# Order of the first loads, larger portions of the edge count, and the place of the check and the split in a GNN and LSTM kernel

## The chip, the cores and the metric

The kernel runs as one program on one core of a Trainium2 chip. The metric is the device time of one execution in microseconds (us); the time of a kernel is the median of several runs. Five engines each take their own instructions strictly in the order in which the program lists them: PE (TensorE: matrix products, with weight loads listed apart as PEld), DVE (VectorE), ACT (ScalarE), POOL (GpSimd) and SP (SyncE, which issues transfers). They wait for each other through semaphores.

## What is computed

```python
def _gcn2_layer(h, h0, src, dst, norm, w1, w2, b, layer):
    beta = float(np.log(LAMBDA / layer + 1.0))
    x = h * norm
    agg = jax.ops.segment_sum(x[src], dst, num_segments=h.shape[0])
    agg = agg * norm
    f, f0 = agg * (1.0 - ALPHA), h0 * ALPHA
    return relu((1-beta)*f + beta*(f @ w1) + (1-beta)*f0 + beta*(f0 @ w2) + b)
...
h = layernorm(x) @ fc_w.T + fc_b                     # x: 1250 rows of 512
norm = clip(degree_of(dst), 1) ** -0.5               # 20000 edges, dst sorted
x = x + layer2(layer1(h))
x = x + lstm(layernorm(x))                           # 1250 steps, hidden size 512
```

A linear layer with a layer norm ahead of it, two graph layers over 20000 edges, and an LSTM over the 1250 rows, with residual sums. Only the part ahead of the first graph layer is touched by the change.

## The kernel before

The 1250 rows stand in T = 10 tiles of 128 partitions by 512. The sum over edges is made as a matrix product with an adjacency matrix of counts, `adj`, which the kernel builds itself on PE: for each of 160 groups of 125 edges, DVE makes two one-hot matrices, `ob` (line 287, source within a tile) and `od` (line 289, target and source tile), and PE multiplies them into one of 32 blocks of 40 target nodes in PSUM (line 303). A block is opened by a product with zeros (line 300). When its last group is in, it is closed (`close_block`, lines 194 to 199): ACT copies it into `adj`, and then DVE reduces it into `S`, the counts for each source tile. There are four PSUM buffers for blocks (`acc`), two for transposes (`psT`), two for products (`psM`, line 207), and eight buffers for one-hot matrices, which is two batches of four groups. `count(n)` (line 338) multiplies batch n, then has DVE make the one-hots of batch n + 2, then closes blocks.

In the first stage PE, DVE and ACT follow an order written out by hand (`manual_schedule`, line 240). A loop over slots s = 0 to 13 (line 358) takes tile s through these steps, a slot apart: PE transposes the normed tile (`xT`); PE multiplies it by the transposed weights `fcT` (`product`, lines 163 to 167, called in line 373) and DVE adds the bias into `h` (line 380); PE transposes `h` (line 378); PE makes two products with `w2` (line 389); DVE adds a bias to each of the two and so frees the two `psM` buffers, at the head of the next slot (lines 366 to 368). Between the steps stand three calls of `count`, one batch each, so that the 40 batches fill slots 0 to 12 and a part of slot 13.

Ahead of the loop DVE converts the edge lists, computes `low` and `key` from them (lines 246 to 275), makes the one-hots of two batches, and takes the layer norm statistics of tiles 0 and 1 (`stats(0, 2)`); `stats(2, 4)` stands in slot 0 and `stats(4, 10)` in slot 1. Each `stats` has one square root on ACT in its middle (line 88).

Transfers: the edge lists on SP and ACT; the rows of tile i on SP for even i and on ACT for odd i, two transfers a tile (`load_rows`, line 112), and four small ones on SP for the last four partitions (`load_last_rows`). POOL issues `fc_w` (1 MB), a bias, the two `w2` (1 MB each) and two biases, and makes `ids_f` (line 237) after them. A transfer on SP or ACT uses one of eight semaphores in turn and so waits until the eighth transfer before it has landed.

After the loop, with no hand-written order, come: the largest entry of `S` (line 432), the degrees as ten products of `S` with a column of ones (`count_edges`, line 397), the number of edges that were not counted (`missing`, lines 436 to 442), `norm` (line 403), and the split of the first layer's input, `h * norm`, into three bf16 planes for each tile (`split_input`, line 420: ACT writes the high plane, DVE the rest, ACT the middle plane, DVE the low one). Four of the ten tiles are split there. Then every engine reads `missing` into a register (line 446) and branches (line 858): with a missing edge to `general()`, otherwise, as here, to `fast()`, which lies behind it. There SP and POOL load the LSTM's input weights `Wx` (line 474), the other six tiles are split (line 674), and PE runs the first layer's sum over edges, `agg` (line 685): for each of four column blocks, 90 products over tiles in the order 6, 7, 8, 9, 0, 1, 2, 3, 4, 5, three planes each.

Of the kernel before, what the change touches and what calls it, by code (L numbers as in the profile page):

```python
# [17 lines left out]
ALPHA = 0.1  # L18
# [20 lines left out]
def gnn_lstm_kernel(  # L39
# [44 lines left out]
    def rsqrt(pool, v, name):  # L84

        w = v.shape[1]
        s = pool.tile([R, w], F32, name=name + "_s")
        nc.scalar.activation(s, v, AF.Sqrt)
        r = pool.tile([R, w], F32, name=name + "_r")
        nc.vector.reciprocal(r, s)  # L90
        q = pool.tile([R, w], F32, name=name + "_q")
        nc.vector.tensor_mul(q, r, r)
        nc.vector.tensor_mul(q, q, v)
        nc.vector.tensor_scalar(q, q, -0.5, 1.5, OP.mult, OP.add)
        nc.vector.tensor_mul(r, r, q)
        return r
# [4 lines left out]
    nc.vector.memset(ones, 1.0)  # L101

# [9 lines left out]
    def load_rows(i, dst):  # L112


        for p0, p1 in ((0, 16), (16, P - 1)):
            (nc.scalar if i % 2 else nc.sync).dma_start(
                dst[4 * p0:4 * p1, i, :],
                bass.AP(tensor=x.tensor, offset=x.offset + (LEN * p0 + 4 * i) * D,
                        ap=[[LEN * D, p1 - p0], [D, 4], [1, D]]))

    def load_last_rows(dst, fill):

        def rows(r, i0, i1, first, n):
            nc.sync.dma_start(dst[R - 4 + r:R - 4 + r + n, i0:i1, :],
                              bass.AP(tensor=x.tensor, offset=x.offset + first * D,
                                      ap=[[D, n], [4 * D, i1 - i0], [1, D]]))
# [19 lines left out]
    def layernorm_scale(pool, mv, name):  # L146
        ve = pool.tile([R, mv.shape[1]], F32, name=name + "_v")
        nc.vector.tensor_scalar(ve, mv[:, :, 1], EPS, None, OP.add)
        return rsqrt(pool, ve, name)
# [36 lines left out]
    with ExitStack() as gnn_stack:  # L186
# [6 lines left out]

        def close_block(p, i, dst):
# [6 lines left out]
        with tc.tile_pool(name="prep", bufs=1) as prep, \  # L201
# [13 lines left out]
            for i in range(T):  # L215
                load_rows(i, xt)
                if i == 0:
                    load_last_rows(xt, fill=True)
            fcw = prep.tile([128, KD, D], F32, name="fcw")
            nc.gpsimd.dma_start(fcw, fc_w.rearrange("(a p) i -> p a i", p=128))  # L220
            biases = []
            for name, v in (("fcb", fc_b), ("b1", b_1), ("b2", b_2)):
                b = prep.tile([R, D], F32, name=name)
                biases.append(b)
            fcb, *bl = biases
            nc.gpsimd.dma_start(fcb, row_bcast(fc_b, R))
            w2 = []
            for i, v in enumerate((w2_1, w2_2)):
                w = prep.tile([128, KD, D], F32, name=f"w2_{i}")
                nc.gpsimd.dma_start(w, v.rearrange("(k p) n -> p k n", p=128))  # L230
                w2.append(w)
            for b, v in zip(bl, (b_1, b_2)):
                nc.gpsimd.dma_start(b, row_bcast(v, R))
# [4 lines left out]
                           allow_small_or_imprecise_dtypes=True)  # L238

            with tc.manual_schedule(engines={mybir.EngineType.PE, mybir.EngineType.DVE,  # L240
                                             mybir.EngineType.Activation}):

# [11 lines left out]
                e_src, e_dst = ends  # L254
                none = edges.tile([ER, BW * T], F16, name="none")
# [54 lines left out]

                mv = prep.tile([R, T, 2], F32, name="mv")
                rstd = prep.tile([R, T], F32, name="rstd")
                nmr = prep.tile([R, T], F32, name="nmr")

                def stats(t0, t1):
                    for t in range(t0, t1):
                        layernorm_stats(work, mv, t, xt[:, t, :])
                    r = layernorm_scale(prep, mv[:, t0:t1, :], f"ln{t0}")
                    nc.vector.tensor_copy(rstd[:, t0:t1], r)
                    nc.vector.scalar_tensor_tensor(nmr[:, t0:t1], mv[:, t0:t1, 0], -1.0, r,  # L320
                                                   op0=OP.mult, op1=OP.mult)

# [9 lines left out]
                n_batch = EC // BATCH  # L332

# [4 lines left out]
                def count(n):  # L338
                    closed = []
                    for c in range(n * BATCH, min((n + 1) * BATCH, EC)):  # L340
                        closed += count_group(c)
                    onehots(n + 2)
                    for p, i in closed:
                        close_block(p, i, adj[:, :, :, 4 * i:4 * i + 4])

                onehots(0)
                onehots(1)
                stats(0, 2)
# [7 lines left out]
                normed(0)  # L356
                n = 0
                for s in range(T + 4):
                    if s < T:
                        xTs[s] = transposed(work, psT, xns.pop(s), "xT")  # L360
# [8 lines left out]
                    if n < n_batch:  # L369
                        count(n)  # L370
                        n += 1
                    if 0 <= s - 1 < T:
                        ps_h[s - 1] = product(psM, xTs.pop(s - 1), fcT)
                    if n < n_batch:
                        count(n)
                        n += 1
# [4 lines left out]
                    if n < n_batch:  # L381
                        count(n)
                        n += 1
# [6 lines left out]
                assert n == n_batch and not blocks  # L390


        deg = gnn.tile([R, T], F32, name="degs")
        norm = gnn.tile([R, T], F32, name="norms")
        norm9 = gnn.tile([R, T], F32, name="norm9")

        def count_edges(psD):
            pd = psD.tile([R, T], F32, name="deg")
            for t in range(T):
                nc.tensor.matmul(pd[:, t:t + 1], S[:, t, :], ones, start=True, stop=True)  # L400
            nc.vector.tensor_copy(deg, pd)

        def degree_norm(pool):
            nc.vector.tensor_scalar(deg, deg, 1.0, None, OP.max)
            r = rsqrt(pool, deg, "norm")
            nc.vector.tensor_copy(norm, r)
            nc.vector.tensor_scalar(norm9, norm, 1.0 - ALPHA, None, OP.mult)

        def split(v, rest, hi, mid, lo, scale=None):

            if scale is None:
                nc.scalar.copy(hi, v)
                nc.vector.tensor_sub(rest, v, hi)
            else:
                nc.scalar.activation(hi, v, AF.Copy, scale=scale)  # L415
                nc.vector.scalar_tensor_tensor(rest, v, scale, hi, op0=OP.mult, op1=OP.subtract)
            nc.scalar.copy(mid, rest)
            nc.vector.tensor_sub(lo, rest, mid)

        def split_input(pool, t, v, scale=None):  # L420
            rest = v if scale is None else pool.tile([R, D], F32, name="rest")
            split(v, rest, *(planes[:, t, i, :] for i in range(3)), scale=scale)

        chunks = [(6, 4), (0, 4), (4, 2)]
        order = [t for t0, n in chunks for t in range(t0, t0 + n)]
        assert sorted(order) == list(range(T))

        AHEAD = 4
        with tc.tile_pool(name="deg_ps", bufs=1, space=PSUM) as psD, \
                tc.tile_pool(name="deg_sb", bufs=2) as sbD:  # L430
            most = sbD.tile([R, 1], F32, name="most")
            nc.vector.tensor_reduce(most, S.rearrange("b i r -> b (i r)"),
                                    mybir.AxisListType.X, OP.max)
            nc.vector.tensor_scalar(most, most, 256.0, None, OP.is_gt)
            count_edges(psD)
            row = sbD.tile([R, 1], F32, name="row")
            nc.vector.tensor_reduce(row, deg, mybir.AxisListType.X, OP.add)
            nc.vector.tensor_sub(row, row, most)
            pn = psD.tile([1, 1], F32, name="total")
            nc.tensor.matmul(pn, row, ones, start=True, stop=True)  # L440
            missing = sbD.tile([1, 1], I32, name="missing")
            nc.vector.tensor_scalar(missing, pn, -1.0, float(E), OP.mult, OP.add)
            degree_norm(gnn)
            for t in order[:AHEAD]:
                split_input(sbD, t, h[:, t, :], norm[:, t:t + 1])
            n_missing = nc.values_load(missing, min_val=0, max_val=E + R)
# [35 lines left out]
        def load_x_again():  # L482
            load_last_rows(h, fill=False)
            for t in order:
                load_rows(t, h)
# [12 lines left out]
        def rstd_of(pool, t0, n):  # L498
            r = layernorm_scale(pool, mv2[:, t0:t0 + n, :], f"lx{t0}")
            nc.vector.tensor_copy(rstd2[:, t0:t0 + n], r)  # L500
# [94 lines left out]
        def general():  # L595


            with tc.tile_pool(name="any", bufs=1) as anyp, \
# [23 lines left out]
                count_edges(any_ps)  # L622
# [40 lines left out]
        def layers():  # L663
            with tc.tile_pool(name="gcn_all", bufs=1) as gcn1, \
# [8 lines left out]

                for t in order[AHEAD:]:
                    split_input(gcn, t, h[:, t, :], norm[:, t:t + 1])
# [216 lines left out]
```

## Time and profile before

| | us |
|---|---|
| median of 3 runs (1155.21 to 1156.94) | 1156.25 |
| the profiled execution | 1157.69 |
| its span, first to last instruction | 1155.9 |
| first stage, up to the last product of the edge count | 194.04 |
| check and branch, up to the first `agg` product | 203.89 |
| end of the first layer's `agg` | 278.60 |
| the second layer's `agg` | 312.99 to 377.84 |
| LSTM, from about | 557 |
| PE busy | 1025.9 (89%) |
| DVE busy | 519.3 (45%) |
| ACT busy | 344.4 (30%) |

A line of the timeline has start, duration, engine, line, operation, what it writes and reads, the count, and in brackets how long the engine stood idle before it and what ended that. A line of the chain of waits has a start, a duration and the work that the end of the program hung on then. fp32 products are recorded as two passes: one `product` of four is recorded as eight. "Granted clock" is the share of the throttle; a lower rate of the products themselves is seen only in their spacing.

### The profile page before, as it was taken

The page shows a single profiled execution, that of the slowest core. Times are in us where ns is not written, and L with a number is a line of the kernel's source. Part 1 is how long each engine was busy: PE and PEld are TensorE (multiplying, and loading weights), DVE is VectorE, ACT ScalarE, POOL GpSimd, SP SyncE. Part 2 cuts the span into 40 slices and gives each one's busy share as a digit, 9 for nine tenths or more (in the row PEclk, how much of TensorE's full clock was granted, in tenths as well). Part 3 has the DMA queues.
Part 4 walks back from the last instruction along what each step waited for, and adds up shares of the span by engine and source line. Part 5 has one row for each costly group of instructions (what it writes and reads, how often), then busy time and mean ns, then how long its engine had stood idle before and what let it go on. Part 6 is the DMA issues. An engine that isn't in the chain of part 4 may idle for free.

```text
span 1155.9 us, 27516 instructions
## 1 busy us (share of the span) xinstructions
PE 1025.9 (89%) x11340; PEld 535.2 (46%) x11356; DVE 519.3 (45%) x1775; ACT 344.4 (30%) x1284; POOL 69.8 (6%) x123
## 2 busy tenths in 40 slices
PE   2999997799999999999788888888888888888886
PEld 1555544355455444444344444444444444444443
DVE  4956665401500665555444444444434444443444
ACT  2312212412500023333333333333333333333332
POOL 1000000300000281000000000000000000010011
PEclk9999999799999999999999999999999999999999
DMA  8000000800300175222632323232322333333331
GB/s 233 1 1 1 1 1 2 256 1 1 89 1 1 69 168 181 109 110 109 199 97 84 97 84 98 84 98 84 94 87 87 95 88 94 102 97 102 102 102 21
DMA packets 41466, 96.22 MB, mean 83 GB/s; under 512 B 6125, under 2 KB 21846, under 8 KB 39928
## 3 DMA queue, kind: packets, MB, share of 16 engines
q1 hardware_dynamic: 35012, 77.59, 22.3%
q0 software_dynamic: 4496, 14.09, 4.2%
q10 hardware_dynamic: 1819, 2.65, 0.8%
q8 instruction: 92, 1.51, 0.6%
q14 instruction: 47, 0.38, 0.1%
HBM read 71.93 MB, written 19.76 MB: 79 GB/s over the span
## 4 chain that ended last, share of the span: by engine, by line
PE 67%; DVE 16%; ACT 9%; issue 4%; DMA 3%; POOL 0%; DVEq 0%; ACTq 0%; SPq 0%
PE gates L540 28%; PE psM L166 15%; PE agg L685 11%; PE psM L510 10%; DVE pr L553 3%; ACT th L556 3%; DVE hT L558 3%; DVE hh L557 3%; DVE cg L554 3%; ACT cg L547 3%; PE acc L303 2%; ACT sg L549 2%; DMA base<-in_x_dram 2%; DMA bx<-in_L_ffn_b_i_dram 1%; PE psT L155 1%
## 5 line engine op out<-in xcount | busy, mean ns | idle before, releaser
L540 PE MATMUL gates<-Wh,hT 128*32 128x256 f32 x8320 | 482.5, 383 | 75.2 <-DVE hT L558 75.2
L540 PEld LDWEIGHTS gates<-Wh,hT 128*32 128x32 f32 x8320 | 244.7, 110 | 287.1 <-DVE hT L558 151.9
L553 DVE TENSOR_TENSOR pr<-sg,cg 128x128 f32<-128x128 f32 x260 | 70.6, 272 | 223.9 <-ACT sg L549 223.8
L685 PE MATMUL agg<-adj,planes 128*128 128x512 bf16 (+1 forms) x704 | 134.6, 352 | 10.0 <-ACT planes L415 7.2
L510 PE MATMUL psM<-Wx,xT 128*128 128x512 f32 x320 | 138.7, 594 | 1.5 <-ACT xT L160 1.5
L547 ACT ACTIVATE cg<-gates 128x64 f32<-128x64 f32 x260 | 58.2, 224 | 249.2 <-PE gates L540 245.6
L556 ACT ACTIVATE th<-cg 128x64 f32<-128x64 f32 x260 | 66.7, 256 | 138.6 <-DVE cg L554 138.6
L685 PEld LDWEIGHTS <-planes 128*128 128x128 bf16 x720 | 71.8, 100 | 73.0 <-ACT planes L415 7.6
L557 DVE TENSOR_TENSOR hh<-so,th 128x64 f32<-128x64 f32 x260 | 58.6, 225 | 86.4 <-ACT th L556 86.0
L510 PEld LDWEIGHTS psM<-Wx,xT 128*128 128x128 f32 x320 | 60.4, 190 | 76.8 <-issue 72.9
L558 DVE STREAM_TRANSPOSE hT<-hh 128x64 f32<-128x64 f32 x260 | 63.8, 246 | 27.9 <-DVE hh L557 0.9
L166 PE MATMUL psM<-w,hT 128*128 128x512 f32 x160 | 70.9, 596 | 0.0
L549 ACT ACTIVATE sg<-gates 128x128 f32<-128x128 f32 x260 | 70.5, 271 | 0.2
L554 DVE TENSOR_TENSOR cg<-pr 128x64 f32<-128x64 f32 x260 | 58.5, 225 | 8.9
L806 POOL TENSOR_TENSOR base<-base,hh 128x128 f32<-128x128 f32 x40 | 18.4, 461 | 693.0 <-issue 533.4
L551 ACT ACTIVATE so<-gates 128x64 f32<-128x64 f32 x260 | 59.8, 230 | 0.0
L532 PE MATMUL gates<-xs,sel 96*32 96x256 bf16 x1040 | 52.5, 272 | 4.2 <-DMA xs<-xp_d 4.2
L303 PE MATMUL acc<-od,ob 125*128 125x400 f16 (+22 forms) x360 | 47.9, 260 | 9.0 <-DVE od L289 8.2
L289 DVE TENSOR_SCALAR od<-ids,key 125x820 f16<-125x820 f16 (+42 forms) x160 | 55.6, 347 | 0.0
L287 DVE TENSOR_SCALAR ob<-ids,low 125x128 f16<-125x128 f16 x160 | 39.5, 247 | 16.3 <-PE acc L303 16.0
L166 PEld LDWEIGHTS psM<-w,hT 128*128 128x128 f32 x160 | 29.7, 190 | 34.0 <-issue 33.0
L303 PEld LDWEIGHTS <-ob 125*128 125x128 f16 x360 | 29.7, 98 | 31.6 <-issue 12.7
(154 smaller groups left out, 663.6 us busy)
## 6 DMA issues: line engine op xcount, KB each, us to landing
xs<-xp_d SPq DMA_DIRECT2D x130, 384.0 KB, 3.2
xp_d<-planes SPq DMA_DIRECT2D x10, 1536.0 KB, 5.4
w<-in_L_gnn_w_dram POOLq DMA_DIRECT2D x4, 1024.0 KB, 12.8
xp_d<-adj POOLq DMA_DIRECT2D x1, 1440.0 KB, 7.8
base<-x SPq DMA_DIRECT2D x20, 64.0 KB, 2.3
base<-x POOLq DMA_DIRECT2D x20, 64.0 KB, 2.6
fcw<-in_L_gnn_fc_w_dram POOLq DMA_DIRECT2D x1, 1024.0 KB, 8.6
out_dram<-base SPq DMA_DIRECT2D x12, 64.0 KB, 2.2
```

Of the source, the lines that this page charges most:

```text
L166: nc.tensor.matmul(p, lT[:, k, :], rhs[:, k, :], start=(k == 0), stop=(k == KD - 1))
L303: nc.tensor.matmul(blocks[i][:, (d0 - i * BW) * T:(d1 - i * BW) * T], ob, od[:, (d0 - lo) * T:(d1 - lo) * T], start=False, stop=last)
L510: nc.tensor.matmul(p, yT[:, k, :], Wx[:, k, j, :, :], start=(k == 0), stop=(k == KD - 1))
L540: nc.tensor.matmul(ps[s][32 * j:32 * (j + 1), :, :], hT[b // 2][:, b % 2, :], Wh[:, b, j, :, 64 * s:64 * (s + 1)], start=False, stop=(b == 3))
L547: nc.scalar.activation(cg[:, 1, :], p[:, 3, :], AF.Tanh)
L549: nc.scalar.activation(sg, p[:, 0:2, :], AF.Sigmoid)
L553: nc.vector.tensor_mul(pr, sg, cg)
L554: nc.vector.tensor_add(cg[:, 0, :], pr[:, 0, :], pr[:, 1, :])
L556: nc.scalar.activation(th, cg[:, 0, :], AF.Tanh)
L557: nc.vector.tensor_mul(hh[:, m], so, th)
L558: nc.vector.transpose(hT.rearrange("p b c -> p (b c)"), hh[:, m])
L685: nc.tensor.matmul(p[:, :n * R], planes[:, k, pl, f * 128:(f + 1) * 128], adj[:, k, t0:t0 + n, :].rearrange("b i r -> b (i r)"), start=(k ...
```

## The change

Loads: `fc_w` goes first on POOL, then `ids_f`, then the three biases. All rows of x go on SP, tiles 0 and 1 first, then 2 and 3, then tiles 4 to 9 together in eight transfers; behind them the two `w2`, also on SP. The four small transfers go on ACT. A square root of a constant on ACT comes ahead of them. `stats(0, 2)` and `normed(0)` move ahead of the one-hots and of `ids`. `rsqrt` writes its last product where it is wanted, so that a copy goes.

Counting: instead of three batches in each slot there are 3 in slot 0, 4 in slots 1 to 8 (1, 2 and 1), 3 in slot 9 and 2 in slot 10.

Check and split: they move into slots 10 to 13, behind those slots' products, in the hand-written order, and all ten tiles are split there. The tiles that they use move to other pools.

```diff
+    warm = keep.tile([128, 1], F32, name="warm")
+    nc.scalar.activation(warm, ones, AF.Sqrt)
...
+        def count_edges(pd):
+            for t in range(T):
+                nc.tensor.matmul(pd[:, t:t + 1], S[:, t, :], ones, start=True, stop=True)
+            nc.vector.tensor_copy(deg, pd[:, :T])
+
+        def row_totals():
+            nc.vector.tensor_reduce(most, S.rearrange("b i r -> b (i r)"),
+                                    mybir.AxisListType.X, OP.max)
+            nc.vector.tensor_scalar(most, most, 256.0, None, OP.is_gt)
+            nc.vector.tensor_reduce(row, deg, mybir.AxisListType.X, OP.add)
+            nc.vector.tensor_sub(row, row, most)
+
+        def total(pn):
+            nc.tensor.matmul(pn, row, ones, start=True, stop=True)
+            nc.vector.tensor_scalar(missing, pn, -1.0, float(E), OP.mult, OP.add)
...
             xt = base1
-            for i in range(T):
-                load_rows(i, xt)
-                if i == 0:
-                    load_last_rows(xt, fill=True)
             fcw = prep.tile([128, KD, D], F32, name="fcw")
             nc.gpsimd.dma_start(fcw, fc_w.rearrange("(a p) i -> p a i", p=128))
...
+            load_rows(0, 2, xt)
+            load_last_rows(xt, nc.scalar, fill=True)
+            load_rows(2, 4, xt)
+            load_rows(4, T, xt)
...
+                stats(0, 2)
                 none = edges.tile([ER, BW * T], F16, name="none")
...
+                normed(0)
                 onehots(0)
                 onehots(1)
-                stats(0, 2)
...
+                per_slot = [(1, 1, 1)] + [(1, 2, 1)] * 8 + [(1, 2, 0), (1, 1, 0)]
                 for s in range(T + 4):
+                    c0, c1, c2 = per_slot[s] if s < len(per_slot) else (0, 0, 0)
...
                     if 0 <= s - 4 < T:
                         for l, p in enumerate(ps_b.pop(s - 4)):
                             nc.vector.tensor_add(base[l][:, s - 4, :], p, bl[l])
-                    if n < n_batch:
-                        count(n)
-                        n += 1
+                    count(c0)
                     if 0 <= s - 1 < T:
                         ps_h[s - 1] = product(psM, xTs.pop(s - 1), fcT)
...
+                    count(c1)
                     if 0 <= s - 2 < T:
                         hTs[s - 2] = transposed(prep2, psT, h[:, s - 2, :], "hT")
                     if 0 <= s - 1 < T:
                         nc.vector.tensor_add(h[:, s - 1, :], ps_h.pop(s - 1), fcb)
...
+                    count(c2)
...
                     if 0 <= s - 3 < T:
                         hT = hTs.pop(s - 3)
                         ps_b[s - 3] = [product(psM, hT, w2[l]) for l in range(2)]
...
+                    if s == T:
+                        count_edges(psT.tile([128, KD, R], F32, name="psT")[:, 0, :])
+                        row_totals()
+                        degree_norm(prep)
+                    if s == T + 1:
+                        total(psT.tile([128, KD, R], F32, name="psT")[:1, 0, :1])
+                    for t in order[slice(*{T: (0, 2), T + 1: (2, 5), T + 2: (5, 8),
+                                           T + 3: (8, T)}.get(s, (0, 0)))]:
+                        split_input(prep2, t, h[:, t, :], norm[:, t:t + 1])
+        n_missing = nc.values_load(missing, min_val=0, max_val=E + R)
...
-                for t in order[AHEAD:]:
-                    split_input(gcn, t, h[:, t, :], norm[:, t:t + 1])
```

Also moved: before the second layer, x is loaded again into `h` in 20 transfers, all on SP now, where SP and ACT had ten each.

## The prediction

> **What bounds the kernel now.** I read the chain of waits first. From 41 us to the end it is almost all PE, so time is won only where PE stands still. That is the case ahead of 41 us and around 200 us, the two places that the change touches. The timeline of the start shows why:
>
> ```profile
> 17.02 0.17 DVE L90 RECIPROCAL ln_r<-ln_s 128x2 f32<-128x2 f32 x1 [1.88 <-ACT ln_s L88]
> 24.95 0.69 DVE L143 BATCH_NORM_STATS2 bnst<-base 128x6 f32<-128x512 f32 x1 [6.71 <-DMA base<-in_x_dram]
> 39.08 1.21 PE L303 MATMUL acc<-od,ob 125*128 125x120 f16 x4 [1.99 <-DVE od L289]
> ```
>
> DVE waits 1.88 us for a square root (a table load on ACT stood in between; the same step at 27.17 waits 0.27), then 6.71 us for tile 2, and has the one-hots that PE lacks only from 38.62 on. I call that start of the one-hots behind `stats(4, 10)` X; it is 38.62 now. The timeline from 194 us on shows the other place:
>
> ```profile
> 194.02 1.59 DVE L197 TENSOR_REDUCE S<-acc 128x40 f32<-128x400 f32 x3
> 195.65 1.49 DVE L432 TENSOR_REDUCE most<-S 128x1 f32<-128x1280 f32 x1
> 195.66 2.39 PE L400 MATMUL deg<-ones,S 128*128 128x1 f32 x20 [1.62 <-DVE S L197]
> 198.94 0.15 DVE L442 TENSOR_SCALAR missing<-total 1x1 int32<-1x1 f32 x1 [0.20 <-PE total L440]
> 203.89 0.61 PE L685 MATMUL agg<-adj,planes 128*128 128x512 bf16 x1 [4.99 <-ACT planes L415]
> 214.75 1.94 ACT L415 ACTIVATE planes<-h,norms 128x512 bf16<-128x512 f32 x3 [8.70 <-DMA Wx<-in_L_ffn_W_i_dram]
> 217.95 4.45 PE L685 MATMUL agg<-adj,planes 128*128 128x512 bf16 x12 [1.71 <-ACT planes L417]
> ```
>
> The last product of the count ends at 194.04 and `agg` begins at 203.89: 9.85 us. The high plane was ready at 201.0, so the 4.80 from `missing` (199.09) to 203.89 are PE's register read and branch. ACT's branch took 8.70, beside the loads of `Wx`. Then `agg` itself: 203.89 to 278.60 is 74.71, the second layer's same products take 64.85 (312.99 to 377.84), so 9.86 are lost: 2.16 and 1.71 in waits, the rest because a product of `agg` takes about 0.37 from 217.95 to 222.4 and from 203.89 to 209.9, against 0.18 later. So after a stretch of little work PE runs for up to 6.0 us at half rate, which costs 3.0; at the start, 0.86 against 0.43 from 30.95 to 35.4 cost 2.2.
>
> **The loads.** Gone from DVE's path up to X: 6.71 for tile 2, 1.61 of the table load (1.88 - 0.27), 0.3 for three small copies: 8.6. The table load now stands at ACT's start, where ACT has only an edge list and four small transfers to issue. New: `stats(0, 2)` stands ahead of `low`, `key` and the one-hots, so that everything on DVE queues behind tiles 0 and 1. DVE is free at 5.98 and takes tile 0's 0.87 first, so tile 1 is late if it lands after 6.85. The transfer view of 3 to 8 us says how fast rows come beside POOL's queue:
>
> ```profile
> q0 software_dynamic: 263, 1.04, 65.6%
> q1 hardware_dynamic: 76, 0.12, 14.8%
> q10 hardware_dynamic: 111, 0.19, 14.0%
> ```
>
> In the chain tile 0's second part, issued at 1.92, lands at 11.4. In the changed kernel q0 holds 1.8 MB instead of 3.9, and q1 has the whole 0.5 MB of tiles 0 and 1 in one line. At q1's share against q0 (18% of 272 GB/s) these land at about 10.7; unhindered under 6.85. I take 9.5, nearer to the row: 2.65 late. **Start: -6.0** (bounds -8.6, and -4.1 at 11.4).
>
> [...]
>
> What else moves in the queues. SP issues 1 + 16 + 2 transfers at 0.78 each, the fifth of its row transfers and later ones waiting for the eighth before. Tiles 2 to 9 (2 MB, at 250 GB/s or so behind tile 1) are due at X - 13.3 = 19 (tiles 2 and 3) and at X - 6.4 = 26, and land by about 12 and 20. The `w2` behind them (24, 28) are wanted on ACT at about 32 and 38. If they were late, ACT would hold up the next `xT`, and PE with it. The first bias comes behind `ids_f` on POOL, wanted only at the first add, 4 behind X. Covered, at nothing.
>
> **Larger portions.** The work is the same; its spacing is not. At X the one-hots take DVE 0.33 to 0.39 a group. In slots 1 to 3 PE now wants 10 batches ahead of its first two `w2` products instead of 7. Adding DVE's rows (10 batches 14.5, two adds 1.4, identity blocks 1.8, closes 1.1) puts those products at X + 18.9, where they now stand at 52.67 = X + 14.05; the three batches more are worth 2.7 on PE. **+2.2** (0 to 4).
>
> Later PE is full: between 41 and 194 it is busy for 149.0 of 153 us, and the waits view gives the rest to one wait:
>
> ```profile
> PE acc L300 <- DVE S L197: 3.9, 5, 1.0
> ```
>
> With four PSUM buffers and one-hots 80 nodes wide, each batch from the 22nd on opens a block whose buffer the batch before it gave back; and on DVE the close stands behind 2 us of one-hots. Where a product (3.4) lies between two batches this is covered. Where only a transpose does, the wait is 0.14 now (142.1). In the new slots 5 to 9 two batches touch and a third follows behind one transpose: batch start to close is 3.0 (139.07 to 142.05), and the next batch's opening comes 2.5 after it. So 0.5 to 0.6, eight times: 4.4 instead of 3.9. **+0.5** (-2 to +2.5).
>
> **Check and split.** This is the step that decides. A PE product needs a free `psM` buffer, there are two, and DVE gives them back by the bias adds at the head of the next slot. DVE takes its list in order. In slot 10 the list is: degrees, `row_totals`, `degree_norm`, the split of two tiles; only then, in slot 11, the adds. I count from the end of the ten degree products:
> - copy, four small operations and `most`: 0.7 + 1.5; square root to `norms` 1.3 (198.77 to 200.05), hand-over 0.1: the split begins at 3.6.
> - a tile: high plane 0.65 (ACT), rest 0.71 (DVE), middle 0.62 (ACT), low 0.65 (DVE), each on the one before; the next tile's high plane stands behind the middle one on ACT, so 2.15 a tile. Tile 7's low plane ends at 8.6, the first add at 9.3.
> - PE has one transpose (0.5) and then **waits 8.9**, to 9.4. The two products take 6.9 and, at half rate at first, 2.4 more (18.7), then `total` (18.9).
> - DVE's next entry is `missing`, which waits for `total`. Behind it stand three tiles and the next two adds: 19.2 + 2 x 2.15 + 2.1 + 0.7 = 26.3. PE **waits 7.5** again, and then has 6.9 + 2.4.
> - PE's branch: 4.8 as now (bounds 3.7, which SP needed, 199.09 to 202.82, and ACT's 8.7). The `Wx` loads start only after the last split, 5 us behind PE's last product, so that I take the quiet value.
>
> From the count to `agg`, beyond the four products and the transpose that the stretch has in either kernel: degrees 2.4, `total` 0.2, waits 8.9 and 7.5, half rate 4.9, branch 4.8: 28.7 instead of 9.85, **+18.9**. In `agg` all planes come in time (the last ones 6 us after PE's last product, wanted 13 us into `agg`), so of the 9.86 lost only one ramp at half rate stays, 3.0: **-6.9**.
>
> [...]
>
> **Hidden or unchanged.** `w1` lands some 28 us after `Wx` begins (202.8 to 230.7), that is about 30 us into `agg`, wanted after 65. ACT's and DVE's own branch beside `Wx` (8.7 to 9.7) is over before the first `agg` block is copied, 16 us in. The reload of x is wanted behind 378, and 20 issues on SP behind 313 are 16 us.
>
> **Sum:** -6.0 + 2.2 + 0.5 + 18.9 - 6.9 = +8.7 on the profiled execution's 1157.69 (span 1155.9 and 1.8 around it): 1166.4. That execution is 1.44 above the median of the runs; on the median, 1156.25, it is **1164.9**.
>
> **Rivals.**
> 1. *It does what its words say, faster.* If DVE gave `psM` back before PE asks (the adds done by 0.5 and by 18.9 of the count above), both waits (16.4) and their ramps (4.9) vanish: 8.7 - 21.3 = -12.6, 1143.6. For it: DVE has only 23.7 of 39 us of work between 155 and 194. Against it: the order of the list, with the adds behind two tiles and then behind `missing`. 7 in 100.
> 2. *No ramp.* PE kept its rate over the 1.99 ahead of 39.08; if it keeps it here too, 4.9 and 3.0 go: +0.8, 1157.0, no difference. Against it: 203.89. 15 in 100.
> 3. *Slower still.* Rows at 11.4 (+1.9) and a PE branch like ACT's, 8.7 (+3.9): +14.5, 1170.7. For it: q0's share. Against it: `Wx` starts behind PE's branch. 18 in 100.
>
> The forecast keeps 60 in 100, with 1159 to 1170 from the bounds of its terms. The range goes from 1156, just under rival 2, to 1172, just over rival 3, which leaves out rival 1 and the ends. About 0.2% (2.3 us) is what a measurement here can tell from no change: faster 9, same 18 (rival 2 and the low end of the forecast), slower 73 in 100.
>
> **What would show it.** X between 30 and 35. PE idle twice for 7 us or more between the degree products and `agg`, the releaser DVE's bias add; the products behind it at 0.86 instead of 0.43. `missing` ahead of three splits on DVE. `agg` without waits, near 68. I am wrong if PE runs through slots 11 to 13, if the gaps leave the rate whole, or if X stays above 36.

## The result and the profile after

The changed kernel takes 1168.72 us (median of 4 runs, 1167.32 to 1172.81) against 1155.73 for the kernel before in the same comparison (1154.96 to 1156.94): a ratio of **1.0117**, 95% interval 1.009 to 1.0144. The profiled execution is the slowest of the four, 1172.81 with a span of 1171.0; the span before was 1155.9. So the trace has to explain +15.1, of which about 13 is typical.

The same milestones, read off the timelines of the profiled executions (us from the start of the span; X is the start of the one-hots behind `stats(4, 10)`, "layer 1" is the first product behind `agg`, `gates` the first product of the LSTM, `far` DVE's last instruction):

| kernel | X | agg begins | layer 1 | gates | far | far to end | span |
|---|---|---|---|---|---|---|---|
| before | 38.62 | 203.89 | 278.44 | 560.92 | 1152.13 | 3.8 | 1155.9 |
| after | 34.42 | 216.24 | 286.85 | 570.01 | 1161.41 | 9.6 | 1171.0 |
| difference | -4.2 | +12.4 | +8.4 | +9.1 | +9.3 | +5.8 | +15.1 |

**The start** of the changed kernel, DVE's timeline (in brackets the idle time ahead and what ended it):

```profile
10.50 0.69 DVE L152 BATCH_NORM_STATS2 bnst<-base 128x6 f32<-128x512 f32 x1 [4.46 <-DMA base<-in_x_dram]
11.72 0.69 DVE L152 BATCH_NORM_STATS2 bnst<-base 128x6 f32<-128x512 f32 x1 [0.30 <-DMA base<-in_x_dram]
20.94 0.69 DVE L152 BATCH_NORM_STATS2 bnst<-base 128x6 f32<-128x512 f32 x1
34.42 0.25 DVE L356 TENSOR_SCALAR ob<-ids,low 125x128 f16<-125x128 f16 x1
```

Tile 2 (20.94) costs no wait any more, where 6.71 stood before. In its place DVE stands 4.46 us for tile 0, and begins tile 1 at 11.72 instead of 6.85: 4.87 late. X is 4.2 earlier.

**The check and the split**, PE's timeline from the end of the count to `agg`:

```profile
178.65 2.29 PE L213 MATMUL psT<-ones,S 128*128 128x1 f32 x20
180.79 0.74 PE L164 MATMUL psT<-ident,h 128*128 128x128 f32 x4
190.01 9.52 PE L175 MATMUL psM<-w,hT 128*128 128x512 f32 x16 [8.48 <-DVE base L431]
199.46 0.19 PE L224 MATMUL psT<-ones,row 128*1 128x1 f32 x2
206.73 9.68 PE L175 MATMUL psM<-w,hT 128*128 128x512 f32 x16 [7.08 <-DVE base L431]
216.24 32.61 PE L694 MATMUL agg<-adj,planes 128*128 128x512 bf16 x180
```

PE stands still twice, and both times DVE's bias add (`base`, line 431) releases it. DVE's own timeline says why the add is late: it is behind the splits (lines 239 and 241), and these behind `missing`, which waits 9.13 us for PE.

```profile
189.28 0.68 DVE L431 TENSOR_TENSOR base<-psM,b 128x512 f32<-128x512 f32 x1
...
199.69 0.15 DVE L225 TENSOR_SCALAR missing<-psT 1x1 int32<-1x1 f32 x1 [9.13 <-PE psT L224]
199.76 0.73 DVE L239 SCALAR_TENSOR_TENSOR rest<-h,norms,planes 128x512 f32<-128x512 f32 x1
...
205.90 0.68 DVE L431 TENSOR_TENSOR base<-psM,b 128x512 f32<-128x512 f32 x1
```

The windows view gives the granted clock of these stretches (the columns are the busy times of PE, PEld, DVE, ACT and POOL, then PEclk, the share of the transfers, GB/s):

```profile
181.50:189.50 8.00, 0.03 (x1) 0.00 (x0) 5.53 (x16) 3.66 (x7) 0.00 (x0) 0.50 0.00 0
190.00:199.50 9.50, 9.49 (x18) 3.94 (x18) 0.56 (x1) 0.00 (x0) 0.00 (x0) 0.75 0.01 2
206.80:216.20 9.40, 9.40 (x16) 3.90 (x17) 5.09 (x8) 3.72 (x6) 0.00 (x0) 0.73 0.01 3
217.00:249.00 32.00, 31.86 (x177) 17.23 (x176) 3.76 (x9) 3.77 (x4) 10.40 (x14) 1.00 0.80 231
252.60:258.00 5.40, 5.29 (x20) 2.38 (x20) 0.35 (x2) 1.90 (x5) 0.00 (x0) 0.68 0.00 0
```

In the wait the clock is at 0.50, and the products behind it run at 0.75 on average, half of their time at half rate. `agg` itself starts at full rate, directly behind the last product: PE's branch costs nothing here. The trace's uncounted records show it all the same: PE's sequencer, which issues the products ahead of their execution, reads `missing` at 207.26 and branches from 207.85 to 211.22 (3.37), while the products that it has already issued run until 216.40. But there is a new wait in `agg`, with a half rate (0.68) behind it. ACT's and PE's timelines, together:

```profile
245.52 1.91 ACT L180 ACTIVATE w<-w 128x2048 f32<-128x2048 f32 x1 [25.01 <-DMA w<-in_L_gnn_w_dram]
250.11 1.91 ACT L180 ACTIVATE w<-w 128x2048 f32<-128x2048 f32 x1 [2.68 <-DMA w<-in_L_gnn_w_dram]
251.92 2.58 ACT L700 COPY h<-agg 128x512 f32<-128x512 f32 x6
```

```profile
252.54 34.47 PE L694 MATMUL agg<-adj,planes 128*128 128x512 bf16 x180 [3.68 <-ACT h L700]
```

ACT scales both `w1` ahead of its first copy of an `agg` block. `w1` lands behind `Wx`, so the six PSUM buffers of `agg` fill up and PE waits 3.68.

**The end.** Both kernels end a fixed step after `far`, but not the same one. The page of the changed kernel begins with its span, and the timeline ends with `far`:

```profile
span 1171.0 us, 27480 instructions
```

```profile
1161.41 0.15 DVE L832 TENSOR_SCALAR far<-pc 1x1 int32<-1x1 f32 x1 [0.28 <-PE pc L830]
```

The 9.6 us behind it hold no counted work. The trace's uncounted records show POOL's closing steps in them, which are the last to end (start, us):

```
before  INC_SWDGE_SEM 1153.20 0.49   DRAIN 1153.72 1.29   span 1155.9
after   INC_SWDGE_SEM 1162.49 1.65   DRAIN 1164.17 6.03   span 1171.0
```

That is 5.9 us more, and nothing in the diff is near it.

### The profile page after: what moved, and what is told of

Its sections match the earlier page's. It is cut to its first block, busy times and chain, and to the rows that moved or that the text cites. A ratio compares the mean times of both kernels' runs of the same rounds, so it can differ in the third digit from the quotient of the medians.

```text
span 1171.0 us, 27480 instructions
## 1 busy us (share of the span) xinstructions
PE 1032.3 (88%) x11356; PEld 538.1 (46%) x11356; DVE 518.5 (44%) x1768; ACT 344.1 (29%) x1285; POOL 68.0 (6%) x121
## 3 DMA queue, kind: packets, MB, share of 16 engines
q0 software_dynamic: 3952, 12.00, 3.3%
## 4 chain that ended last, share of the span: by engine, by line
PE 63%; DVE 18%; ACT 9%; issue 4%; DMA 3%; POOL 0%; DVEq 0%; SPq 0%; ACTq 0%; POOLq 0%
PE gates L551 27%; PE psM L175 15%; PE psM L521 10%; PE agg L694 8%; DVE pr L564 3%; ACT th L567 3%; DVE hT L569 3%; DVE cg L565 3%; DVE hh L568 3%; ACT cg L558 2%; ACT sg L560 2%; PE acc L372 2%; DMA w<-in_L_gnn_w_dram 1%; DVE od L358 1%; DMA bx<-in_L_ffn_b_i_dram 1%
## 5 line engine op out<-in xcount | busy, mean ns | idle before, releaser
L564 DVE TENSOR_TENSOR pr<-sg,cg 128x128 f32<-128x128 f32 x260 | 70.6, 272 | 224.6 <-ACT sg L560 224.0
L694 PE MATMUL agg<-adj,planes 128*128 128x512 bf16 x720 | 132.0, 347 | 3.8 <-ACT h L700 3.7
L175 PE MATMUL psM<-w,hT 128*128 128x512 f32 x160 | 75.6, 628 | 15.6 <-DVE base L431 15.6
L372 PEld LDWEIGHTS <-ob 125*128 125x128 f16 x360 | 30.2, 98 | 31.0 <-issue 11.4
```

The source lines that it names most:

```text
L175: nc.tensor.matmul(p, lT[:, k, :], rhs[:, k, :], start=(k == 0), stop=(k == KD - 1))
L372: nc.tensor.matmul(blocks[i][:, (d0 - i * BW) * T:(d1 - i * BW) * T], ob, od[:, (d0 - lo) * T:(d1 - lo) * T], start=False, stop=last)
L564: nc.vector.tensor_mul(pr, sg, cg)
L694: nc.tensor.matmul(p[:, :n * R], planes[:, k, pl, f * 128:(f + 1) * 128], adj[:, k, t0:t0 + n, :].rearrange("b i r -> b (i r)"), start=(k ...
```

## The experiments

The theory after the trace: the two waits come from the order of DVE's list, the half rate from the waits, the wait in `agg` from `w1` behind `Wx`, and the closing drain from something in the new start. Rivals: the larger portions are dear; the work is too much for DVE and ACT in any order; the drain is chance. Each ratio below is against the kernel before, run in the same comparison (its median was between 1155.7 and 1158.1 in these).

### e1_adds_first: the bias adds ahead

```diff
-                    if 0 <= s - 4 < T:
-                        for l, p in enumerate(ps_b.pop(s - 4)):
-                            nc.vector.tensor_add(base[l][:, s - 4, :], p, bl[l])
+                    if 0 <= s - 4 < T - 3 or s == T + 3:
+                        add_base(s - 4)
...
                     if s == T:
+                        add_base(T - 3)
                         count_edges(psT.tile([128, KD, R], F32, name="psT")[:, 0, :])
...
                     if s == T + 1:
+                        add_base(T - 2)
                         total(psT.tile([128, KD, R], F32, name="psT")[:1, 0, :1])
```

`add_base(t)` makes the two bias adds of tile t.

> The changed kernel with the bias adds of the last slots moved in DVE's list: those of tile 7 ahead of the degrees (in slot 10), those of tile 8 ahead of `missing` (in slot 11); tile 9's stay. Theory (PE loses 8.5 and 7.1 us because the order of DVE's list returns `psM` late): from the end of the degree products D the transpose and the products of tile 8 run at once (D + 7.4), the first add of tile 8 ends at D + 9.2, so one wait of about 1.8 is left, no half rate, and `agg` starts at D + 16.2 instead of D + 35.3: -19.1. But the last split then ends at D + 28, 12 us behind the start of `agg` (now 5), so `Wx` and `w1` come 7 us later against it and the wait for ACT's copies inside `agg` grows from 3.7 to about 10: in all -12, 1156 to 1157. Rival (the work itself, not its order, is too much for DVE and ACT beside the products): the waits move behind the last product as waits of `agg` for planes, -5 at the most, 1164 or more.

Measured: **1158.08**, ratio 1.0008 (0.9995 to 1.0021). PE's timeline:

```profile
181.69 8.73 PE L175 MATMUL psM<-w,hT 128*128 128x512 f32 x16
190.35 0.19 PE L224 MATMUL psT<-ones,row 128*1 128x1 f32 x2
190.54 7.10 PE L175 MATMUL psM<-w,hT 128*128 128x512 f32 x16
197.48 32.61 PE L699 MATMUL agg<-adj,planes 128*128 128x512 bf16 x180
238.86 11.39 PE L699 MATMUL agg<-adj,planes 128*128 128x512 bf16 x49 [8.76 <-ACT h L705]
```

Both waits are gone and `agg` begins at 197.48 (197.1 expected), with the same work on all engines: the order was the cause. And 8.76 us come back inside `agg`, since `Wx` and `w1` start only behind the last split, which is now later against `agg`. Of the 18.8 won at the start of `agg`, 5.6 are given back 40 us later (`agg` lasts 76.2 here, 70.6 in the changed kernel).

### e8_adds_w1: and `w1` ahead of `Wx`

```diff
-                Wx, bx = load_wx(late_w)
-                layers()
+                Wx, bx = wx_tiles(late_w)
+                layers((Wx, bx))
...
                 w1 = load_w1(gcn1)
+                load_wx(None, wx)
```

`wx_tiles` allocates the tiles without loading them.

> The edit of the adds and `w1` loaded ahead of `Wx`. Theory (order of DVE's list, and then the late `w1`, which ACT scales ahead of its first copy of `agg`): `agg` starts 19.1 earlier, and the wait of 3.7 with the 1.9 of half rate behind it is gone: -24.7, 1144. Rival (the copies wait for something else than `w1`): as with the adds alone, 1156. Rival (the order is not the cause): 1163 or more.

Measured: **1147.16**, ratio 0.9906 (0.9881 to 0.9931). `agg` runs without a stop:

```profile
196.63 65.06 PE L703 MATMUL agg<-adj,planes 128*128 128x512 bf16 x360
```

It lasts 64.9 where the changed kernel's lasts 70.6. Between the two medians lie 21.6 us, 3 less than the 24.7 expected; but they come from two comparisons, and by the two ratios (1.0117 and 0.9906) it is 24.4, with intervals of about 3 on each. So no shortfall is shown.

### e5_w1_first: `w1` ahead of `Wx` alone

The second edit of e8_adds_w1, on the changed kernel.

> The changed kernel with `w1` loaded ahead of `Wx` on POOL's queue. Theory (ACT's list has the scaling of both `w1` ahead of its first copy of `agg`, `w1` comes behind `Wx`, and PE waits 3.7 for the copies and then runs at half rate for 1.9 of loss): wait and half rate gone, -5.6, 1163.1. Rival (the wait is ACT's own, or a later load takes it over): -1 to +1.

Measured: **1166.22**, ratio 1.0083 (1.0059 to 1.0108). In the profile `agg` lasts 64.9 and has no wait, as expected, but the time is only 2.5 lower (3.9 by the two ratios, whose intervals overlap). The wait differs between executions: 3.7 in the changed kernel's, 1.0 and 1.2 in those of e4_busy_pe and e7_rows_first, where the order of these loads is the same; the second `w1` came 33.9 us into `agg` in the first, 31.2 and 31.4 in the others. Behind the waits of 1.0 and 1.2 the second half of `agg` takes 32.94, about as the first half (32.61); behind 3.68 it takes 34.47. So the term is 1 to 6 us, an estimate from these three executions.

### e2_start_alone and e3_start_portions: the parts of the change

Both have the check and the split behind the loop again, as in the kernel before (four tiles split there, six ahead of `agg`). The first also has the old portions:

```diff
-                    if s == T:
-                        count_edges(psT.tile([128, KD, R], F32, name="psT")[:, 0, :])
-                        row_totals()
-                        degree_norm(prep)
...
+            for t in order[:AHEAD]:
+                split_input(sbD, t, h[:, t, :], norm[:, t:t + 1])
...
-                per_slot = [(1, 1, 1)] + [(1, 2, 1)] * 8 + [(1, 2, 0), (1, 1, 0)]
+                per_slot = [(1, 1, 1)] * 12 + [(1, 1, 1), (1, 0, 0)]
```

> The new start (order of loads, statistics of two tiles first, table loaded early) alone: three single batches a slot, and the check and the split behind the loop, as before the change. Theory: the one-hots behind stats(4, 10) start at 34.4 instead of 38.6, and nothing behind takes the 4.2 back: 1151.5. Rival (an earlier start is lost later, since PE is full from there on or the end is set elsewhere): 1155 to 1156, as before.

> The new start and the larger portions, with the check and the split behind the loop as before the change. Theory: the portions cost 3.1 (2.7 forecast) over the start alone: 1154.6. Rival (the larger portions are a main part of the loss): 1158 or more. A rival on the other side: portions cost nothing, 1151.5.

Measured: **1157.93**, ratio 1.0000 (0.9987 to 1.0013), and **1157.78**, ratio 0.9994 (0.9978 to 1.001). The milestones:

| kernel | X | agg begins | layer 1 | far | far to end | span |
|---|---|---|---|---|---|---|
| e2_start_alone | 33.45 | 201.38 | 272.94 | 1146.52 | 9.7 | 1156.2 |
| e3_start_portions | 33.72 | 199.67 | 273.28 | 1147.43 | 9.7 | 1157.1 |

The new start is worth 5.6 us at `far` (one execution each), and the closing drain takes 5.9 of them back: a real gain that the time does not show. The time is the rival's, and of its two reasons it is the end that is set elsewhere: the gain is whole at `far` and is lost behind it. The portions are within what can be told from nothing (0.6 against X at `far`, nothing in the medians).

### e10_before_w2_on_sp: one line of the start

```diff
-                nc.gpsimd.dma_start(w, v.rearrange("(k p) n -> p k n", p=128))
+                nc.sync.dma_start(w, v.rearrange("(k p) n -> p k n", p=128))
```

This is the kernel before, with the two `w2` on SP's queue.

> The kernel before the change with one edit: the two `w2` are loaded on SP's queue instead of POOL's (3952 packets on q0). Theory: everything up to `far` within 1 us of before, and the closing drain as in the changed kernel, so that it is slower by 5.8: 1161.5 to 1162. Rival (the drain depends on another part of the start): no change, 1156.

Measured: **1158.18**, ratio 1.0003 (0.9990 to 1.0016). The drain came as expected: 1.65 and 6.03, 9.6 from `far` to the end. But "everything up to `far` as before" was wrong: X is 33.45, as early as with the whole new start, and `far` at 1148.01 is 4.1 earlier. DVE's timeline:

```profile
16.29 0.17 DVE L90 RECIPROCAL ln_r<-ln_s 128x2 f32<-128x2 f32 x1 [1.28 <-ACT ln_s L88]
18.18 0.69 DVE L143 BATCH_NORM_STATS2 bnst<-base 128x6 f32<-128x512 f32 x1 [0.68 <-DMA base<-in_x_dram]
```

The wait for tile 2 falls from 6.71 to 0.68 because 2 MB less lie on POOL's queue, with the old order of rows and of statistics. So all of the start's gain at X comes with this one line, and at `far`, in one execution each, 4.1 of 5.6; the two medians, 1158.18 here and 1157.93 in e2_start_alone, are not apart.

### e9_adds_w1_pool2, e11_adds_w1_pool1: more transfers on POOL's queue

```diff
-                    (nc.sync if k % 2 else nc.gpsimd).dma_start(
+                    (nc.sync if k % 2 and not (k == 3 and g in (2, 3)) else nc.gpsimd).dma_start(
                         Wx[:, k, :, g, :],
```

The second kernel has `g == 3` alone. Both stand on e8_adds_w1.

> The adds moved and `w1` first (1147.2 so far), and two of the eight `Wx` parts of SP's queue on POOL's instead, which brings POOL's queue (q0) from 3952 packets in the records back to 4496, as before the change. Theory (the program's last step, POOL's closing drain, took 6.03 us and the step ahead of it 1.65 in every kernel whose q0 has 3952, against 1.29 and 0.49 before the change, because of what POOL's queue has carried): from `far` to the end 3.8 instead of 9.6, 1141.3. Rival (the closing drain is long for another reason in the new start: SP's transfers, the early table load, the order of loads): 9.6 still, 1147.

> As the kernel with two `Wx` parts more on POOL's queue, but one part: 4224 packets on q0. If the closing drain grows or shrinks in steps with what the queue carried since some wrap (4096 would be one), it is short here too, 3.8 or less from `far` to the end; if it falls evenly from 3952 to 4496, 6.7; if it needs all that POOL's queue carried before the change, 9.6.

Measured: **1142.15**, ratio 0.9873 (0.9850 to 0.9896), and 1142.50 in one run (1141.3 expected for the first). From `far` to the end 3.8 and 3.7. A `Wx` part brought 80 packets, not 272, so q0 had 4112 and 4032. With 4032, below 4096, the drain was already the short one, so that a limit of 4096 packets is out. What orders all runs is the number of transfers that POOL issued:

| transfers issued by POOL | kernels | q0 packets | INC_SWDGE_SEM | DRAIN |
|---|---|---|---|---|
| 72 | e7 | 3680 | 1.63 | 5.95 |
| 73 | after, e1 to e6, e8, e10 | 3952 | 1.65 | 6.03 |
| 74 | e11 | 4032 | 0.41 | 0.97 |
| 75 | before, e9, e12 | 4496, 4112, 3920 | 0.49 | 1.29 |

The nine kernels with 73 transfers agree to 0.01 us, so the drain is not chance. The number that SP issued does not order them: it is 273 in e10_before_w2_on_sp, with the long drain, and 283 in e9_adds_w1_pool2, with the short one.

### e7_rows_first and e12_rows_first_too: rows ahead of `fcw`

```diff
-            nc.gpsimd.dma_start(fcw, fc_w.rearrange("(a p) i -> p a i", p=128))
             load_rows(0, 2, xt)
+            nc.sync.dma_start(fcw, fc_w.rearrange("(a p) i -> p a i", p=128))
```

> The changed kernel with `fcw` on SP's queue behind the rows of tiles 0 and 1, instead of on POOL's queue from the start. Theory (POOL's queue, with 65.6% of the engines, starves SP's): tile 0 lands at about 7.5 instead of 10.5, DVE's wait of 4.46 falls to about 1.5, and the one-hots behind stats(4, 10) start 3 earlier: 1165.7. Rival (the rows come late by their own latency or issue): tile 0 still at 10 or later, no change or worse, 1168.7 or more.

Measured: **1168.09**, ratio 1.0104 (1.0079 to 1.0129). Tile 0 lands at 9.17 instead of 10.50 (7.5 expected) and X is 32.69, 1.7 earlier; the ten kernels with the changed kernel's loads have X between 33.45 and 35.07. The time is not to be told from the changed kernel's. The same edit on e9_adds_w1_pool2, with a third `Wx` part so that POOL issues 75 transfers again:

> As the kernel with the adds moved, `w1` first and two `Wx` parts more on POOL's queue, and besides `fcw` on SP's queue behind the rows of tiles 0 and 1 and a third `Wx` part on POOL's queue, so that POOL issues 75 transfers as before the change. So far the closing drain took 5.95 and 6.03 with 72 and 73 transfers issued by POOL, 0.97 and 1.29 with 74 and 75, and 1.29 with 75 whether q0 had 4112 or 4496 packets. Theory (the number of POOL's transfers sets it): 1.29 and 3.8 from `far` to the end; the one-hots behind stats(4, 10) start at 32.7 instead of 35.1 (34.4 in the changed kernel), so 1140 to 1141. Rival (which transfers, or their bytes): a long drain, 1146.

Measured: **1142.89**, ratio 0.9894 (0.9875 to 0.9913), X 34.15, tile 0 at 9.39, a closing drain of 1.29 with 3920 packets. The number of transfers foretold the drain. X and the time missed what was expected (32.7, 1140 to 1141): DVE waits another 1.14 for tile 1, and the time is not below that of e9_adds_w1_pool2. The rows do not come at 7.5: with nothing of `fcw` ahead of them they land at 9.2 to 9.4, against 9.5 to 11.0 with it. So most of their lateness is not due to `fcw` on POOL's queue; what it is due to is not shown.

### e4_busy_pe: PE kept busy in the waits

```diff
+                    if s in (T + 1, T + 2):
+                        idle = psT.tile([128, KD, R], F32, name="psT")
+                        for _ in range(18 if s == T + 1 else 14):
+                            nc.tensor.matmul(idle.rearrange("p k r -> p (k r)"), ident, w2[0][:, 0, :],
+                                             start=True, stop=True)
```

> The changed kernel with 18 and 14 products whose result nothing reads (0.43 us each) on PE where it waits for the bias adds of tiles 7 and 8. Theory (the products behind a wait run at half rate because PE stood idle): both waits become busy time, the products of tiles 8 and 9 take 6.9 each instead of 9.5 and 9.7, -5.3, 1163.4. Rival (these products are slow for another reason, operands or PSUM): no change, 1168.7.

Measured: **1176.41**, ratio 1.0174 (1.0149 to 1.0200). I had sized the idle work wrongly: one such product is two of the 0.43 rows, so that the 18 took 15.65 us in a wait of 8.5. The time is thereby no test. The clock is one. Windows view of this kernel, the products of tiles 8 and 9:

```profile
196.00:202.60 6.60, 6.60 (x16) 2.66 (x14) 0.00 (x0) 0.00 (x0) 0.00 (x0) 1.00 0.00 0
215.00:221.70 6.70, 6.70 (x17) 2.83 (x16) 1.53 (x3) 1.24 (x2) 0.00 (x0) 1.00 0.02 5
```

Clock 1.00, and each pair takes 7.03 instead of 9.52 and 9.68: the lower clock costs 2.5 and 2.7, and the rival (operands or PSUM) is out. Not all of the first need come from the wait: in e1_adds_first the same pair takes 8.73 with no wait ahead of it.

### e6_total_late: the branch in the open

```diff
-                    if s == T + 1:
+                    if s == T + 3:
                         total(psT.tile([128, KD, R], F32, name="psT")[:1, 0, :1])
```

> The changed kernel with `total` and `missing` moved from slot 11 to slot 13, behind the last products. Theory: the splits of slot 11 no longer stand behind `missing`, so the second wait of 7.1 and its half rate go and the last product ends at about 206.4; but now PE's register read and branch follow `missing` directly and cost about 4.8 again, with a half rate behind them of 2 to 3: `agg` at about 211.5 instead of 216.2; `Wx` begins closer to `agg` and the wait of 3.7 for `w1` goes: in all -8, 1161. Rival (the branch is cheap in the changed kernel because no load runs beside it): `agg` at about 207.5, -13, 1156. Rival (`missing` does not hold DVE up): +4 or more, 1173.

Measured: **1164.54**, ratio 1.0065 (1.0040 to 1.0091). PE's and DVE's timelines:

```profile
190.06 16.60 PE L175 MATMUL psM<-w,hT 128*128 128x512 f32 x32 [8.59 <-DVE base L431]
206.60 0.19 PE L224 MATMUL psT<-ones,row 128*1 128x1 f32 x2
212.24 6.14 PE L694 MATMUL agg<-adj,planes 128*128 128x512 bf16 x23 [5.45 <-DVE planes L241]
```

```profile
207.81 0.14 DVE L225 TENSOR_SCALAR missing<-psT 1x1 int32<-1x1 f32 x1
```

The second wait is gone (`missing` did hold DVE up), and from the end of `missing` (207.95) to `agg` (212.24) PE now needs 4.29, with a half rate behind it: 23 products in 6.14. So the branch has not become cheap: 3.60 of the 4.29 are PE's branch instruction (uncounted, 208.57 to 212.17), and `agg` starts behind it; the planes that the bracket names do not set its start. In the changed kernel the same instruction takes 3.37 and is hidden, because the products issued ahead of it run 5.2 us longer than it does. The value need not be old for that: in e1_adds_first `missing` is written at 191.21, PE branches from 191.84 to 195.64, and the products issued ahead of the branch run on until `agg` begins at 197.48. `agg` came near the 211.5 expected; the time is 3.5 above the 1161 expected.

## Why the prediction came near, step by step

The forecast, 1164.9, is 3.8 too low; the time lies in its range, on the side that was forecast. The sum of +8.7 against +9.3 up to `far` looks better than it was: -5.7 between the count and `agg` met +1.8 at the start, +0.6 in the portions, +3.0 in `agg` and +0.9 behind it. So the sign and the two waits were foreseen, and that the number came so near is luck.

- **Start, -6.0:** -4.2 at X. Tile 1 was begun 4.87 late, and I had taken 2.65; the pessimistic bound (rows at 11.4) was the better value. Of the gain at X, 1.6 is lost again by the last product also in e2_start_alone (X to there 157.0, before 155.4).
- **Larger portions, +2.2 and +0.5:** mis-sized. e3_start_portions has 1.5 more than e2_start_alone from X to the last product. It no longer has the wait of 1.62 for the last close ahead of the degree products, so that between these two kernels nothing is left; but the forecast's 28.7 has no such wait either, so that its 2.7 is to be held against the 1.5. The late waits at the opening of blocks are 3.9, as before (4.4 forecast).
- **Check and split, the waits:** 8.48 and 7.08 for 8.9 and 7.5, released by the add, with `missing` ahead of three splits. Right in size and cause; e1_adds_first shows the cause.
- **Half rate, 4.9:** 2.5 + 2.7 = 5.2 by e4_busy_pe. How long a wait must be to bring it is not shown. A wait of 3.68 in the changed kernel was followed by a clock of 0.68, and waits of 1.0 and 1.2 (e4_busy_pe, e7_rows_first) left it at 1.00; but in e2_start_alone a wait of 2.27 in `agg` was followed by 0.50 (213.4 to 216.0), and the wait of 1.62 ahead of the degree products by 0.61, where the same wait in the kernel before left 1.00.
- **PE's branch, 4.8: this step failed.** I carried the 4.80 of before into another order. There PE has nothing left to run when it branches; here products issued ahead of the branch run until 216.40, and the branch is done at 211.22. It costs 0, and `agg` has no ramp at its start (0 instead of 3.0), since PE never stops. Together 7.8 too dear.
- **"`w1` lands about 30 us into `agg`, wanted after 65": this step failed too.** The landing was nearly right (the two at 29.3 and 33.9 us into `agg`), the need was not: ACT's list has the scaling of `w1` ahead of its first copy of `agg` (as in the kernel before, at 227.63 and 232.47), so it is wanted when six buffers are full, 32.6 us in, with 4 us of scaling ahead. It costs 1 to 6 us.
- **Nothing at the end of the program: this step was missing.** Moving two transfers off POOL's queue made the closing drain 5.9 longer. I priced what the queues carry at the start and not that POOL issues two transfers fewer.

In the profiled execution: -4.2 at X, +3.3 from there to the last product without the waits, 23.1 instead of 9.85 between count and `agg` (+13.2), -3.9 in `agg`, +0.9 from layer 1 to `far`, +5.8 behind it: +15.1. What the other three executions have less, 3.8 to 5.5, is not in a trace; the wait for `w1` is one part that varies.

Rival 1, "it does what its words say", is what e9_adds_w1_pool2 makes of the change: 16 us under before (1142.15 against 1158.1 in that comparison) with two adds, two loads and two issues put elsewhere. Rival 2 (no ramp) is refuted by the clock. Rival 3's time, 1170.7, is close, but only its late rows occurred.

## What to carry to other kernels

Work that is "put beside" another engine's goes into the list of the engine that returns the buffers, so look where the return then stands in it, and what it waits for. When a stretch gets shorter, ask at once what was loaded behind its end and who now asks for it earlier. And look at the last microseconds of the profile too: a change at the start moved the program's end by 5.9.

## What was not expected of the hardware

- **POOL's closing steps went with how many transfers POOL issued**, not with their packets: 7.6 and 7.7 us with 72 and 73, 1.4 and 1.8 with 74 and 75, and the same 1.29 of drain with 75 transfers of 4496, 4112 or 3920 packets. From 72 to 73 they grew by 0.1, from 74 to 75 by 0.4, and between 73 and 74 they fell by 6.3. Only these four numbers were tried, and what makes the fall is not shown.
- **The branch cost PE 4.1 to 4.8 us or nothing.** The instruction took PE 3.4 to 4.0 us in all 14 kernels. It cost 4.1 to 4.8, counted from the value, where PE had nothing left to run (before, e2, e3, e6, e10), and nothing where products issued ahead of it ran longer, even when the value has only just been written (e1_adds_first).
- **The clock also fell without a wait.** In e1_adds_first PE is busy from 176 on, and yet the products behind the ten one-column degree products run at 0.60 for 4.3 us (8.73 for a pair that takes 7.03):

```profile
176.00:181.50 5.50, 5.50 (x31) 3.75 (x30) 1.33 (x4) 0.00 (x0) 0.00 (x0) 1.00 0.01 3
181.70:186.00 4.30, 4.30 (x9) 1.76 (x8) 3.20 (x12) 0.93 (x2) 0.00 (x0) 0.60 0.00 0
```

  In all 14 kernels the trace's record of the clock changed only after whole steps of 3.41 us, and the steps lie differently in each. In e1_adds_first it is 0.50 for one step, 182.18 to 185.59. The degree products take 2.29 us. Where one step holds them whole, the clock falls at its end (the changed kernel, at 181.19 and so before PE stands still at 181.53, and e1, e5, e6, e8, e11). Where the edge of a step cuts them, so that at most 1.98 lie in one, it does not (e4, e9, e12; in e7 it falls a step later, in the wait). These are ten kernels; what it is in a step that lowers the clock behind it is not shown.

- **2 MB on POOL's queue held up rows on SP's and ACT's**: DVE's wait for the third tile fell from 6.71 to 0.68 us when the two `w2` went from it to SP's, with no row moved (e10_before_w2_on_sp).
